# Attention scores of two heads on the two halves of the array's rows, with more buffers for the exponentials, in a fused attention and convolution kernel

## The chip, the cores and the metric

The kernel runs on one core of a Trainium2 chip. The metric is the time of one execution on the device in microseconds, as the median of several executions. Beside the times there is a profile: one execution recorded by the hardware profiler, instruction by instruction, for the engines TensorE (PE; its weight loads are PEld), VectorE (DVE), ScalarE (ACT) and GpSimd (POOL), for the SyncE queue (SP) that issues DMAs, and for the DMA queues.

## The reference

Two layers on an input of 4 images, 128 channels, 64 x 64 pixels, all in float32. The first is self-attention with group normalization, 4 heads of 32 channels, over the 4096 pixels of an image; the second is a residual block of two 3 x 3 convolutions with weights quantized to 3 bits and batch normalization over all images.

```python
# layer 0
x_norm = _group_norm(x, norm_w, norm_b)                   # 8 groups
qkv = einsum('oc,bchw->bohw', qkv_w, x_norm) + qkv_b
q, k, v = split(qkv, 3, axis=1)                           # 4 heads, d = 32
attn = softmax(einsum('bhid,bhjd->bhij', q, k) * d ** -0.5)
out = einsum('bhij,bhjd->bhid', attn, v)
x = x + einsum('oc,bchw->bohw', proj_w, out) + proj_b
# layer 1
out = relu(batchnorm(conv3x3(x, lsq_quantize(w1, alpha1))))
out = batchnorm(conv3x3(out, lsq_quantize(w2, alpha2)))
return relu(out + x)
```

## The kernel before

The attention works on 32 blocks: image b (4 of them) and a chunk of 512 queries qb (8 an image). A block has 32 steps; a step takes 128 keys (kt) and all four heads. For each step TensorE forms the scores s of 128 keys by 512 queries for each head, ScalarE takes their exponential into a tile p of 128 x 2048, TensorE multiplies p with v and accumulates acc over the steps, and p is added up over the steps for the softmax's denominator: most steps by VectorE (r), some by a DMA that accumulates into another tile (rm). The scores are not rounded to the short mantissa of the fast float32 format: q and k are split into a high and a low part, and all four products are summed. Before, the four parts of one head (4 x 32 rows) are stacked on the 128 rows of the array, so one product with K=128 gives one head's scores.

```python
kpool = ctx.enter_context(tc.tile_pool(name="kpool", bufs=NB + 1))        # NB = 8
pss = ctx.enter_context(tc.tile_pool(name="pss", bufs=3, space=PSUM))     # scores, 2 x 512
psa = ctx.enter_context(tc.tile_pool(name="psa", bufs=2, space=PSUM))     # acc, l, po, pk, pq, pv
...
ppool = att.enter_context(tc.tile_pool(name="ppool", bufs=6))
rpool = att.enter_context(tc.tile_pool(name="rpool", bufs=1))

def stack_tile(name):
    return kpool.tile([P, HEADS, FB], F32R, name=name, tag="k")           # 128 x 2048
...
def project_parts(b, j, xin, wide=False):       # q, k, v of one chunk of 512 pixels
    ...
    def parts(what, bias, slot):
        hi = stage.tile([P, FB], F32R, name=f"{what}h{b}_{j}", tag=f"{what}h")
        lo = stage.tile([P, FB], F32R, name=f"{what}l{b}_{j}", tag=f"{what}l")
        nc.scalar.activation(hi, ps[what], AF.Identity, bias=bias)
        nc.vector.scalar_tensor_tensor(lo, ps[what], bias, f32(hi), ALU.add, ALU.subtract)
        nc.sync.dma_start(out=kq[b, j][slot], in_=f32(hi))
        nc.sync.dma_start(out=kq[b, j][slot + 1], in_=f32(lo))
    ...
    return [normalize, lambda: mm("k", P), lambda: parts("k", bk, 0),
            lambda: mm("q", 0), lambda: parts("q", bq, 2), mmv, evac_v]

def load_stack(t, b, j, slots):                 # k: (0, 1, 0, 1), q: (2, 2, 3, 3)
    for s, slot in enumerate(slots):
        nc.sync.dma_start(
            out=f32(t)[s * D : (s + 1) * D, :, :],
            in_=kq[b, j][slot].rearrange("(h d) n -> d h n", d=D))
...
MOVED = range(0, NK - 4, 4)                     # NK = 32

def scores(pair):
    ...
    s = pss.tile([P, 2, FB], F32, name=f"s{n}_{kt}_{half}", tag="s")
    for i in range(2):
        h = 2 * half + i
        nc.tensor.matmul(s[:, i, :], k[:, h, c0 : c0 + P], q[:, h, :], start=True, stop=True)
    nc.scalar.activation(pts[step][:, 2 * half : 2 * half + 2, :], s, AF.Exp, scale=SCALE)

def weights(step):
    ...
    for h in range(HEADS):
        nc.tensor.matmul(acc[n][h * D : (h + 1) * D, :], v[:, kt % KB, h * D : (h + 1) * D],
                         pt[:, h, :], start=(kt == 0), stop=(kt == NK - 1))
    if kt in MOVED:
        if kt == 0:
            msum[n] = rpool.tile([P, HEADS, FB], F32, name=f"rm{n}", tag="rm")
            nc.sync.dma_start(out=msum[n], in_=pt)
        else:
            nc.gpsimd.dma_start(out=msum[n], in_=pt, accum_op=ALU.add)
    elif kt == 2:
        rsum[n] = rpool.tile([P, HEADS, FB], F32, name=f"r{n}", tag="r")
        nc.vector.tensor_tensor(rsum[n], pts[step - 1], pt, ALU.add)
    elif kt > 2:
        nc.vector.tensor_tensor(rsum[n], rsum[n], pt, ALU.add)
```

The end of a block (l: the denominator from r and rm; its reciprocal; po: the output projection) and the projections of the next image's chunks are put between the steps of a block by a list of places; TensorE runs the scores one to two steps ahead of the products with v:

```python
def chunk(b, j, kt, fs, loads):                 # fs: what project_parts returns
    add(kt, "", fs[0])
    add(kt, "q", fs[1])
    add(kt + 1, "", fs[2])
    add(kt + 1, "q", fs[3])
    add(kt + 2, "", fs[4])
    add(kt + 2, "q", fs[5])
    add(kt + 3, "", fs[6])
    ...
# next image's chunks by block: two in blocks 2 and 3, one in 4 to 7
for j, kt in {2: ((0, 13), (1, 22)), 3: ((2, 13), (3, 22)), 4: ((4, 15),), ...
...
run_scores(2)
while at["step"] < steps:
    for s, w in ((3, 1), (3, 2)):
        run_scores(s)
        run_weights(w)
```

The convolutions take bands of 16 rows, two products' groups j of 8 rows each in one PSUM tile of 2 x 512:

```python
for m, (b, g) in enumerate(bandlist):
    ps = done[m] if m < len(done) else conv_tile(i, b, g)
    for j in range(2):
        if m >= len(done):
            conv(ready[i, b, g], ps, j, wq[i])            # 18 products into ps[:, j, :]
        if j == 0:
            prepare(m)
        c = 2 * g + j
        dst = cv[b][:, c * FB : (c + 1) * FB]
        nc.scalar.copy(dst, ps[:, j, :])
        nc.vector.bn_stats(st[:, b * NB + c, :], ps[:, j, :])
```

Of the kernel before, what the change touches and what calls it, by code (L numbers as in the profile page):

```python
# [78 lines left out]
def _fast_body(ctx, tc, x, norm_w, norm_b, qkv_wt, qkv_b, proj_wt, proj_b,  # L79
# [62 lines left out]
    def quant_tasks(pool):  # L142
        tasks = []
        for i, (w, alpha) in enumerate(((w1, alpha1), (w2, alpha2))):
# [19 lines left out]
            for c in range(3):  # L164


                def taps(i=i, c=c, w=w, t=t):
                    wr, q0, qh, ql = (
                        pool.tile([P, FB], F32R, name=f"{n}{i}{c}", tag=tag).bitcast(F32)
                        [:, : 3 * P].rearrange("p (t o) -> p t o", o=P)  # L170
                        for n, tag in (("wr", "kh"), ("q0", "kl"), ("qh", "qh"), ("ql", "ql")))
                    nc.sync.dma_start(out=wr, in_=w[:, 3 * c : 3 * c + 3, :])
                    nc.vector.tensor_scalar(q0, wr, t["inv"], -8.0, ALU.mult, ALU.max)
                    nc.vector.tensor_scalar(q0, q0, 8.0, None, ALU.min)
                    nc.vector.tensor_scalar(qh, q0, SPLIT, None, ALU.add)
                    nc.vector.tensor_scalar(qh, qh, SPLIT, None, ALU.subtract)
                    nc.vector.tensor_tensor(ql, q0, qh, ALU.subtract)
                    nc.vector.scalar_tensor_tensor(wr, qh, t["a_h"], wr, ALU.mult, ALU.subtract)
                    nc.vector.scalar_tensor_tensor(wr, qh, t["a_l"], wr, ALU.mult, ALU.add)
                    nc.vector.scalar_tensor_tensor(wr, ql, t["a_h"], wr, ALU.mult, ALU.add)  # L180
                    nc.vector.scalar_tensor_tensor(wr, ql, t["a_l"], wr, ALU.mult, ALU.add)
                    nc.vector.scalar_tensor_tensor(q0, wr, t["ninv"], q0, ALU.mult, ALU.add)
                    nc.vector.tensor_scalar(q0, q0, QN, QP, ALU.max, ALU.min)
                    nc.vector.tensor_scalar(q0, q0, ROUND, None, ALU.add)
                    nc.vector.tensor_scalar(wq[i][:, 3 * c : 3 * c + 3, :], q0, ROUND, None,
                                            ALU.subtract)

                tasks.append(taps)
# [11 lines left out]
    y0 = [dram.tile([P, N], F32, name=f"y0_{b}") for b in range(B)]  # L200
    att = ExitStack()
# [4 lines left out]
    ppool = att.enter_context(tc.tile_pool(name="ppool", bufs=6))  # L206
    rpool = att.enter_context(tc.tile_pool(name="rpool", bufs=1))

    def stack_tile(name):
        return kpool.tile([P, HEADS, FB], F32R, name=name, tag="k")  # L210
# [50 lines left out]
    kq = {}  # L261
    qs, ks, vs = {}, {}, {}

    def project_parts(b, j, xin, wide=False):
        xn = xpool.tile([P, FB], F32, name=f"xn{b}_{j}", tag="x")
        kq[b, j] = dram.tile([5, P, FB], F32, name=f"kq{b}_{j}")
        ps = {}

        def bank(what):
            if wide:  # L270
                t = pss.tile([P, 2, FB], F32, name=f"p{what}{b}_{j}", tag="s")
                return t[:, 0, :]
            return psa.tile([P, FB], F32, name=f"p{what}{b}_{j}", tag="a")

# [8 lines left out]
        def parts(what, bias, slot):  # L283
            hi = stage.tile([P, FB], F32R, name=f"{what}h{b}_{j}", tag=f"{what}h")
            lo = stage.tile([P, FB], F32R, name=f"{what}l{b}_{j}", tag=f"{what}l")
            nc.scalar.activation(hi, ps[what], AF.Identity, bias=bias)  # L286
            nc.vector.scalar_tensor_tensor(lo, ps[what], bias, f32(hi), ALU.add, ALU.subtract)  # L287
            nc.sync.dma_start(out=kq[b, j][slot], in_=f32(hi))
            nc.sync.dma_start(out=kq[b, j][slot + 1], in_=f32(lo))
# [7 lines left out]
        def evac_v():  # L297
            v = stage.tile([P, FB], F32, name=f"vst{b}_{j}", tag="v")
# [3 lines left out]
            nc.sync.dma_start(out=kq[b, j][4], in_=v)  # L302

        return [normalize, lambda: mm("k", P), lambda: parts("k", bk, 0),
                lambda: mm("q", 0), lambda: parts("q", bq, 2), mmv, evac_v]

    def load_stack(t, b, j, slots):
        for s, slot in enumerate(slots):
            nc.sync.dma_start(
                out=f32(t)[s * D : (s + 1) * D, :, :],  # L310
                in_=kq[b, j][slot].rearrange("(h d) n -> d h n", d=D))

    def load_kv(b, j):
        ks[b, j] = stack_tile(f"k{b}_{j}")
        load_stack(ks[b, j], b, j, (0, 1, 0, 1))
        v = vs[b, j] = vpool.tile([P, KB, P], F32, name=f"v{b}_{j}", tag="v")
        nc.sync.dma_start(out=v.rearrange("p i f -> p (i f)"), in_=kq[b, j][4])

    def load_q(b, j):
        qs[b, j] = qpool.tile([P, HEADS, FB], F32R, name=f"q{b}_{j}", tag="q")  # L320
        load_stack(qs[b, j], b, j, (2, 2, 3, 3))
# [4 lines left out]
    MOVED = range(0, NK - 4, 4)  # L326


    def scores(pair):
# [8 lines left out]
        for i in range(2):  # L338
            h = 2 * half + i
            nc.tensor.matmul(s[:, i, :], k[:, h, c0 : c0 + P], q[:, h, :], start=True, stop=True)  # L340
# [25 lines left out]
    def finish_parts(n):  # L366
# [10 lines left out]
        def total():  # L377
# [5 lines left out]
            t["ls"] = stage.tile([P, FB], F32, name=f"ls{n}", tag="v")  # L383
# [26 lines left out]
    BR = 2 * RB  # L410

    def band_tile(name):
        return (stack_tile(name).rearrange("p h n -> p (h n)")[:, : (BR + 2) * PW]
                .rearrange("p (r w) -> p r w", w=PW))
# [31 lines left out]
    PRE = 3  # L446
    halves = [stack_tile(f"xh{i}") for i in range(2)]
    for j in range(NB):
        eng = (nc.sync, nc.scalar)[j % 2]
        eng.dma_start(out=f32(halves[j // 4])[:, j % 4, :], in_=x_chunk(0, j))  # L450
    st = small.tile([P, NB, 6], F32, name="st0", tag="st")
    for j in range(NB):
        nc.vector.bn_stats(st[:, j, :], f32(halves[j // 4])[:, j % 4, :])
# [3 lines left out]
    def first_chunk(j, wide):  # L457
        return project_parts(0, j, lambda: f32(halves[j // 4])[:, j % 4, :], wide)

    for j in range(PRE):  # L460
        for f in first_chunk(j, True):
            f()
        load_kv(0, j)
        if j == 0:
            load_q(0, 0)

    def schedule(n, before):
# [6 lines left out]
        if before:  # L476
# [5 lines left out]
            add(11, "", before["store"])  # L482
# [5 lines left out]
        def chunk(b, j, kt, fs, loads):  # L488
            add(kt, "", fs[0])
            add(kt, "q", fs[1])  # L490
            add(kt + 1, "", fs[2])
            add(kt + 1, "q", fs[3])
            add(kt + 2, "", fs[4])
            add(kt + 2, "q", fs[5])
            add(kt + 3, "", fs[6])
            if loads:
                add(kt + 3, "", lambda: load_kv(b, j))

        if n == 0:
            for j in range(PRE, NB):  # L500
                chunk(0, j, 4 * (j - PRE), first_chunk(j, False), True)
        if b + 1 < B:
# [12 lines left out]
            for j, kt in {2: ((0, 13), (1, 22)), 3: ((2, 13), (3, 22)), 4: ((4, 15),),  # L515
                          5: ((5, 15),), 6: ((6, 15),), 7: ((7, 15),)}.get(qb, ()):
                xt = {}
                add(kt - 4, "", lambda j=j, xt=xt: xt.update({0: load_x(b + 1, j)}))
                chunk(b + 1, j, kt, project_parts(b + 1, j, lambda xt=xt: xt[0]), False)
# [113 lines left out]
    def layer(i, prepare, done):  # L633

        st = mid.tile([P, B * NB, 6], F32, name=f"st{i}")
        for m, (b, g) in enumerate(bandlist):
            ps = done[m] if m < len(done) else conv_tile(i, b, g)
            for j in range(2):
                if m >= len(done):
                    conv(ready[i, b, g], ps, j, wq[i])  # L640
                if j == 0:
                    prepare(m)
# [3 lines left out]
                nc.vector.bn_stats(st[:, b * NB + c, :], ps[:, j, :])  # L646
# [32 lines left out]
    HN = N // 2  # L679
    res = {}  # L680

    def load_res(b, i):
        if b < B - 1:
            t = mid.tile([P, HN], F32, name=f"res{b}_{i}")
        else:
            t = f32(stack_tile(f"res{b}_{i}")).rearrange("p h n -> p (h n)")
# [3 lines left out]
    def second(m):  # L690
        if m + 2 < len(bandlist):
            relu_band(*bandlist[m + 2])
        if m < 2 * B - 2:
            load_res(m // 2, m % 2)

    a2, c2 = layer(1, second, [])
    for i in range(2):
        load_res(B - 1, i)
    Q = N // 4
    for b in range(B):  # L700
        for j in range(4):
            y = res[b, j // 2][:, (j % 2) * Q : (j % 2 + 1) * Q]
            cs = slice(j * Q, (j + 1) * Q)
# [462 lines left out]
```

## Time and profile before

| | |
|---|---|
| time, median of 3 | 3187.3 us (3182.93 to 3188.45) |
| span of the profiled execution | 3177.3 us, mean granted TensorE clock 0.94 |
| busy: TensorE, VectorE, ScalarE, GpSimd | 2731.6, 2196.2, 2099.9, 184.4 us |
| score products (L340) | 4096, 431 ns each in the mean, 1237.5 us busy |
| products with v (L352) | 8192 records, 1084.7 us busy |
| exponentials (L341) | 2048, 1036 ns each, 1927.5 us busy |
| additions of p by VectorE (L364, L362) | 736 and 32, 2284 and 2292 ns each |
| additions of p by DMA (L359) | 192 of 1024 KB, 7.2 us to landing in the median |
| weight loads of the scores | 4096, 194 ns each |

The busy time of an engine is the union of its instructions. Matmuls are pipelined, so their lengths overlap: what a group of them costs is read from the start of one to the start of the next. In a row of the profile's groups stands the line, the engine, the operation, what it writes and reads, the shape and the count, then the busy time and the mean of one, then the time that the engine stood idle just before and what ended it. The chain is followed back from the last instruction, at each step to what released it. A window's row has the busy time of each engine in one stretch.

### The profile page before, as it was taken

To read this page: it belongs to the slowest core of one execution; us is meant where nothing else is said; L and a number is where in the kernel's file an instruction comes from. 1 tells how busy PE (TensorE), PEld (TensorE's weight loads), DVE (VectorE), ACT (ScalarE), POOL (GpSimd) and SP (SyncE) were. 2 spreads that over 40 slices of the span, in tenths; PEclk is the share of its full clock that TensorE was granted. 3 is DMA by queue.
4 is the path that set the end of the run, shared out by engine and by line. 5 is a ranking of instruction groups with operands and counts; after the bars stand their busy time and mean duration, and the time that the engine had idled before them with its cause. 6 is when DMAs were issued, how large, how long until landed. Compare 5 with 4: busy or idle time off the path is not lost.

```text
span 3177.3 us, 36327 instructions
## 1 busy us (share of the span) xinstructions
PE 2731.6 (86%) x14418; PEld 1226.8 (39%) x14418; DVE 2196.2 (69%) x1445; ACT 2099.9 (66%) x2306; POOL 184.4 (6%) x302
## 2 busy tenths in 40 slices
PE   5898889888998888888898788878978999988785
PEld 2333333333333333333343333333333343356563
DVE  3686767765786677766786676766898888863334
ACT  4586777766876677776786677766867888831223
POOL 1000000000000000000000000000000000000000
PEclk8898999998999999999999899988989999999998
DMA  8766555567665655567565555577545556634003
GB/s 244 174 139 151 121 128 131 123 142 173 142 138 124 148 124 125 127 154 177 130 139 123 126 133 124 128 159 173 129 95 107 127 124 131 133 74 121 10 1 133
DMA packets 155123, 413.70 MB, mean 130 GB/s; under 512 B 49649, under 2 KB 50417, under 8 KB 125249
## 3 DMA queue, kind: packets, MB, share of 16 engines
q0 software_dynamic: 28128, 201.67, 31.4%
q1 hardware_dynamic: 126240, 208.58, 24.1%
q8 instruction: 115, 1.88, 0.2%
q10 hardware_dynamic: 576, 1.05, 0.1%
q14 instruction: 64, 0.52, 0.0%
HBM read 117.64 MB, written 58.72 MB: 56 GB/s over the span
## 4 chain that ended last, share of the span: by engine, by line
PE 53%; DMA 24%; ACT 6%; DVE 6%; issue 5%; ACTq 0%; POOLq 0%; POOL 0%; DVEq 0%; SPq 0%
DMA rm<-p 22%; PE s L340 21%; PE acc L352 20%; PE c L583 8%; ACT p L341 5%; DVE r L364 2%; PE l L381 2%; DMA q<-kq 1%; PE pk L281 1%; PE pv L294 1%; DMA k<-kq 1%; PE pq L281 1%; DVE st L646 1%; DVE res L704 1%; ACT cv L645 1%
## 5 line engine op out<-in xcount | busy, mean ns | idle before, releaser
L341 ACT ACTIVATE p<-s 128x1024 f32<-128x1024 f32 x2048 | 1927.5, 1036 | 668.1 <-PE s L340 405.4
L364 DVE TENSOR_TENSOR r<-r,p 128x2048 f32<-128x2048 f32 x736 | 1680.8, 2284 | 182.6 <-ACT p L341 139.2
L340 PE MATMUL s<-q,k 128*128 128x512 f32 x4096 | 1237.5, 431 | 145.4 <-ACT p L341 121.0
L340 PEld LDWEIGHTS s<-q,k 128*128 128x128 f32 x4096 | 712.8, 194 | 976.9 <-ACT p L341 513.7
L352 PE MATMUL acc<-p,v 128*32 128x512 f32 x8192 | 1084.7, 633 | 0.0
L352 PEld LDWEIGHTS acc<-p,v 128*32 128x32 f32 x8192 | 203.1, 112 | 512.6 <-issue 503.0
L359 POOL DMA_DIRECT2D rm<-p x192 | 164.5, 857 | 2573.3 <-ACT p L341 1493.2
L645 ACT COPY cv<-c 128x512 f32<-128x512 f32 x64 | 37.3, 587 | 275.1 <-PE c L583 257.9
L362 DVE TENSOR_TENSOR r<-p,p 128x2048 f32<-128x2048 f32 x32 | 73.3, 2292 | 187.0 <-PE l L381 187.0
L583 PE MATMUL c<-hi,wq 128*128 128x512 f32 x576 | 155.4, 415 | 52.1 <-DVE st L646 46.1
L646 DVE BATCH_NORM_STATS2 st<-c 128x6 f32<-128x512 f32 x64 | 44.7, 698 | 204.2 <-ACT cv L645 203.8
L287 DVE SCALAR_TENSOR_TENSOR kl<-pk,bk,kh 128x512 fp32r<-128x512 f32 x32 | 24.0, 750 | 190.3 <-ACT kh L286 190.3
L583 PE MATMUL c<-lo,wq 128*128 128x512 f32 x576 | 148.1, 401 | 0.0
L583 PEld LDWEIGHTS c<-hi,wq 128*128 128x128 f32 x576 | 108.2, 193 | 94.5 <-DVE st L646 59.4
L583 PEld LDWEIGHTS c<-lo,wq 128*128 128x128 f32 x576 | 108.7, 189 | 29.4
L281 PE MATMUL pk<-xn,wqkv 128*128 128x512 f32 x64 | 49.3, 862 | 82.0 <-ACT xn L277 82.0
L388 DVE RECIPROCAL rc<-ls 128x128 f32<-128x128 f32 x128 | 114.9, 927 | 2.8 <-ACT ls L384 2.8
L287 DVE SCALAR_TENSOR_TENSOR ql<-pq,bq,qh 128x512 fp32r<-128x512 f32 x32 | 24.0, 749 | 115.3 <-ACT qh L286 115.2
L281 PE MATMUL pq<-xn,wqkv 128*128 128x512 f32 x64 | 42.2, 746 | 58.9 <-DVE kl L287 58.9
L294 PE MATMUL pv<-wqkv,xn 128*128 128x128 f32 x256 | 40.5, 307 | 54.4 <-DVE ql L287 54.4
L294 PEld LDWEIGHTS pv<-wqkv,xn 128*128 128x128 f32 x256 | 36.3, 213 | 69.4 <-DVE ql L287 66.6
L281 PEld LDWEIGHTS pk<-xn,wqkv 128*128 128x128 f32 x64 | 13.1, 242 | 92.8 <-ACT xn L277 92.2
(101 smaller groups left out, 605.8 us busy)
## 6 DMA issues: line engine op xcount, KB each, us to landing
rm<-p POOLq DMA_DIRECT2D x192, 1024.0 KB, 7.4
k<-kq SPq DMA_DIRECT2D x128, 256.0 KB, 7.9
q<-kq SPq DMA_DIRECT2D x128, 256.0 KB, 7.1
rm<-p SPq DMA_DIRECT2D x32, 1024.0 KB, 5.6
x<-in_x_dram SPq DMA_DIRECT2D x80, 256.0 KB, 6.1
kq<-kh SPq DMA_DIRECT2D x32, 256.0 KB, 4.0
kq<-kl SPq DMA_DIRECT2D x32, 256.0 KB, 4.4
kq<-qh SPq DMA_DIRECT2D x32, 256.0 KB, 2.0
```

The lines of the kernel that those rows point to most:

```text
L281: nc.tensor.matmul(ps[what], wqkv[:, o : o + P], xn, start=True, stop=True)
L294: nc.tensor.matmul(ps["v"][:, i * P : (i + 1) * P], xn[:, i * P : (i + 1) * P], wqkv[:, 2 * P : 3 * P], start=True, stop=True)
L340: nc.tensor.matmul(s[:, i, :], k[:, h, c0 : c0 + P], q[:, h, :], start=True, stop=True)
L341: nc.scalar.activation(pts[step][:, 2 * half : 2 * half + 2, :], s, AF.Exp, scale=SCALE)
L352: nc.tensor.matmul(acc[n][h * D : (h + 1) * D, :], v[:, kt % KB, h * D : (h + 1) * D], pt[:, h, :], start=(kt == 0), stop=(kt == NK - 1))
L359: nc.gpsimd.dma_start(out=msum[n], in_=pt, accum_op=ALU.add)
L362: nc.vector.tensor_tensor(rsum[n], pts[step - 1], pt, ALU.add)
L364: nc.vector.tensor_tensor(rsum[n], rsum[n], pt, ALU.add)
L388: nc.vector.reciprocal(rc[:, cs], t["ls"][:, cs])
L583: nc.tensor.matmul(ps[:, j, :].rearrange("p (r w) -> p r w", w=W), w[:, tap, :], part[:, j * RB + kh : j * RB + kh + RB, kw : kw + W], sta ...
L645: nc.scalar.copy(dst, ps[:, j, :])
L646: nc.vector.bn_stats(st[:, b * NB + c, :], ps[:, j, :])
```

## The change

Two heads' scores are formed on the two halves of the array's rows. A k stack now holds, on 64 rows, the high and the low part of one head, and on the other 64 rows those of another; q is given twice, once with its high part on all rows and once with its low part, and the two products are accumulated in PSUM (K=64, four products for a pair of heads where there were two). The k stack is half as wide, and the room goes to p: nine buffers instead of six. Of the 32 steps of a block six instead of seven are added up by DMA. The products of a projection (k, q, v) stand three steps apart and are evacuated two steps later, where they stood one step apart and were evacuated right after. A fourth chunk of the first image is projected before the attention begins, and what is staged there lies in buffers of p. In the convolutions both groups of a band come before their copies, and the statistics are taken from the copy in SBUF instead of from PSUM. The residual is loaded in quarters of an image instead of halves, since the k stacks that serve as its buffers are smaller.

```diff
-    ppool = att.enter_context(tc.tile_pool(name="ppool", bufs=6))
+    ppool = att.enter_context(tc.tile_pool(name="ppool", bufs=9))
 ...
     def stack_tile(name):
-        return kpool.tile([P, HEADS, FB], F32R, name=name, tag="k")
+        return kpool.tile([P, KW], F32R, name=name, tag="k")      # KW = 1188
 ...
-    def load_stack(t, b, j, slots):
-        for s, slot in enumerate(slots):
-            nc.sync.dma_start(
-                out=f32(t)[s * D : (s + 1) * D, :, :],
-                in_=kq[b, j][slot].rearrange("(h d) n -> d h n", d=D))
+    def load_k(b, j):
+        k = ks[b, j] = stack_tile(f"k{b}_{j}")[:, : 2 * FB].rearrange("p (g n) -> p g n", n=FB)
+        for s in range(4):
+            i, part = divmod(s, 2)
+            src = kd[b, j][part].rearrange("(g i d) n -> i d g n", i=2, d=D)
+            nc.sync.dma_start(out=f32(k)[s * D : (s + 1) * D, :, :], in_=src[i])
 ...
     def load_q(b, j):
-        qs[b, j] = qpool.tile([P, HEADS, FB], F32R, name=f"q{b}_{j}", tag="q")
-        load_stack(qs[b, j], b, j, (2, 2, 3, 3))
+        q = qs[b, j] = qpool.tile([P, 2, 2, FB], F32R, name=f"q{b}_{j}", tag="q")
+        src = qd[b, j].rearrange("s (g i d) n -> i g d s n", i=2, d=D)
+        for s in range(4):
+            for g in range(2):
+                nc.sync.dma_start(out=f32(q)[s * D : (s + 1) * D, g, :, :], in_=src[s // 2, g])
 ...
-    MOVED = range(0, NK - 4, 4)
+    MOVED = range(0, NK - 6, 5)
 ...
-        for i in range(2):
-            h = 2 * half + i
-            nc.tensor.matmul(s[:, i, :], k[:, h, c0 : c0 + P], q[:, h, :], start=True, stop=True)
+        for part in range(2):
+            for i in range(2):
+                r = slice(64 * i, 64 * (i + 1))
+                nc.tensor.matmul(s[:, i, :], k[r, half, c0 : c0 + P], q[r, half, part, :],
+                                 start=(part == 0), stop=(part == 1))
 ...
-    PRE = 3
-    halves = [stack_tile(f"xh{i}") for i in range(2)]
+    PRE = 4
+    halves = [ppool.tile([P, HEADS, FB], F32, name=f"xh{i}", tag="p") for i in range(2)]
 ...
-            add(11, "", before["store"])
+            add(12, "", before["store"])
 ...
+        def chunk(kt, fs, gap, wait):
+            add(kt - gap, "", fs[0])
+            for i in range(3):
+                add(kt + gap * i, "q", fs[1 + 2 * i])
+                add(kt + gap * i + wait, "", fs[2 + 2 * i])
 ...
-            for j, kt in {2: ((0, 13), (1, 22)), 3: ((2, 13), (3, 22)), 4: ((4, 15),),
-                          5: ((5, 15),), 6: ((6, 15),), 7: ((7, 15),)}.get(qb, ()):
+            for j, kt in {2: ((0, 13), (1, 22)), 3: ((2, 13), (3, 22)), 4: ((4, 17),),
+                          5: ((5, 17),), 6: ((6, 17),), 7: ((7, 17),)}.get(qb, ()):
 ...
-                chunk(b + 1, j, kt, project_parts(b + 1, j, lambda xt=xt: xt[0]), False)
+                chunk(kt, project_parts(b + 1, j, lambda xt=xt: xt[0]), 3, 2)
 ...
                 if m >= len(done):
                     conv(ready[i, b, g], ps, j, wq[i])
-                if j == 0:
-                    prepare(m)
+            prepare(m)
+            for j in range(2):
                 c = 2 * g + j
                 dst = cv[b][:, c * FB : (c + 1) * FB]
                 nc.scalar.copy(dst, ps[:, j, :])
-                nc.vector.bn_stats(st[:, b * NB + c, :], ps[:, j, :])
+                nc.vector.bn_stats(st[:, b * NB + c, :], dst)
 ...
-    HN = N // 2
+    HN = N // 4
```

## The prediction

> **What bounds the kernel now.** I began with the chain that ended last, on the profile's page, because no engine is full (TensorE 86%, VectorE 69%, ScalarE 66%):
>
> ```profile
> PE 53%; DMA 24%; ACT 6%; DVE 6%; issue 5%; ACTq 0%; POOLq 0%; POOL 0%; DVEq 0%; SPq 0%
> DMA rm<-p 22%; PE s L340 21%; PE acc L352 20%; PE c L583 8%; ACT p L341 5%; DVE r L364 2%; PE l L381 2%; DMA q<-kq 1%; PE pk L281 1%; PE pv L294 1%; DMA k<-kq 1%; PE pq L281 1%; DVE st L646 1%; DVE res L704 1%; ACT cv L645 1%
> ```
>
> Half of the path is TensorE, but the accumulating DMAs (rm<-p) hold 22%. A share is an average, so I cut the attention into its 32 query blocks, at the 32 copies of acc into av (159.1 to 2804.0 us, mean 85.3 us a block), and asked for engine times in single blocks (columns: window, length, busy PE, PEld, DVE, ACT, POOL, clock, DMA share, GB/s):
>
> ```profile
> 234.50:330.40 95.90, 82.00 (x423) 33.51 (x422) 64.40 (x39) 63.98 (x72) 5.18 (x6) 0.91 0.53 127
> 677.40:782.10 104.70, 80.28 (x405) 32.77 (x404) 62.45 (x36) 62.26 (x68) 5.16 (x6) 0.85 0.83 189
> 2591.00:2661.40 70.40, 68.03 (x399) 27.89 (x398) 59.23 (x33) 60.40 (x66) 5.11 (x6) 1.00 0.59 128
> ```
>
> The third is a block of the last image, without projections for a next one: 70.4 us, PE busy nearly throughout, full clock. The first projects two chunks and needs 95.9; the second also loads the next image's k: 104.7. So the floor is TensorE at 70.4, and the rest of the mean (85.3 - 70.4 = 15 us a block) is waiting. The timeline of an undisturbed stretch gives the floor's parts:
>
> ```profile
> 2560.25 1.92 PE L352 MATMUL acc<-p,v 128*32 128x512 f32 x16
> 2562.10 1.66 PE L340 MATMUL s<-q,k 128*128 128x512 f32 x6
> 2562.87 5.60 ACT L341 ACTIVATE p<-s 128x1024 f32<-128x1024 f32 x6 [0.59 <-PE s L340]
> 2563.69 1.06 PE L352 MATMUL acc<-p,v 128*32 128x512 f32 x8
> 2564.69 1.82 PE L340 MATMUL s<-q,k 128*128 128x512 f32 x6
> 2566.44 1.92 PE L352 MATMUL acc<-p,v 128*32 128x512 f32 x16
> ```
>
> From start to start, 16 acc take 1.85, 6 scores 1.59, 8 acc 1.00, 6 scores 1.75: 6.19 us for three steps. ScalarE needs 5.60 and waits 0.59 for PE. 32 steps make 66.0; l and po bring it to 70. The chain inside the 95.9 us block shows the waiting:
>
> ```profile
> 246.56 11.21 DMA rm<-p
> 258.31 7.04 DMA rm<-p
> ...
> 270.84 0.59 ACT kh L286
> 271.45 0.76 DVE kl L287
> 272.26 1.17 PE pq L281 x2
> ...
> 282.82 3.57 PE acc L352 x16
> ```
>
> Two kinds: exponentials' buffers held by accumulating DMAs, and a relay k product, ScalarE, VectorE, q product, during which PE stands. Afterwards the 16 acc took 3.57 instead of 1.85: half clock. In the convolutions the chain repeats:
>
> ```profile
> 2875.86 8.88 PE c L583 x36
> 2884.77 0.59 ACT cv L645
> 2885.39 0.71 DVE st L646
> 2886.14 8.88 PE c L583 x36
> ```
>
> **The Trainium skill.** "TensorEngine Tiling (Array Packing)", Key Properties, says that different tiles load weights and multiply in parallel, and that changing the mode drains the array. The trace agrees for column tiles: the four heads' acc products start some 7 ns apart in single records; no row tile is in it. "TensorE: Matmul & The Clock Gate", Measured speedup vs the span model, has about 4 ns per further tile, and its LDWEIGHTS section says that load time follows columns, not rows; here 128 columns took 194 ns and 32 took 112, so K=64 weights should load no faster. HAM oscillation in that page (idle of some 3 us halves the clock) agrees with the 3.57 above.
>
> **The change part by part.**
> Scores. Per half step, two K=128 products become four of K=64, two per half of the rows. If the halves run together, this is again two rounds of about 0.23 us (single records: 0.228 to 0.236 apart). 32 x 32 x 4 = 4096 rounds; 4 ns for the second tile is +16 us, an estimate from the clock-gate page. Nothing is saved on PE; what is bought is room: k stacks of half the columns pay for three more p buffers, and k loads move half the bytes.
>
> Buffers and DMAs. Six p buffers at about 2.1 us a step cover 12.6 us; an accumulating DMA takes 7.2 us in the median, up to 14.5, after its step and its predecessor. In the 95.9 us block the first one landed at 257.8, 23 us into the block; the exp that reuses its buffer (six steps on, issued about 1.5 steps early) wanted it at 8.5 x 2.1 = 18. With nine buffers and p5 as the first, it is wanted 12.5 steps in, at 70.4/32 = 2.2 a step 27.5 us. Six moved tiles instead of seven come 5 x 2.2 = 11 us apart, above the 7 to 9 us between chained ones in the 70.4 us block. So ScalarE's 220.7 us of waits for rm<-p, and what they drag along, should go. VectorE gets one more add a block: 2.29 x 32 = 73 us, beside PE.
>
> Spaced products. Three steps between k, q and v products with evacuation two steps later: the relay (some 8 us with the halved clock after it) leaves the path, and PE's own part stays: pk 0.86 + pq 0.86 + pv 1.1 + joints 0.4 = 3.2 us a chunk.
>
> Blocks, then: plain 70.3 (the shortest, 2733.7 to 2804.0); with group statistics 71.5, an allowance of 1.2; one chunk 73.5; two chunks 76.7. Images 1 to 3 (less the first block): 2 x 70.3 + 3 x 71.5 + 6 x 76.7 + 12 x 73.5 = 1697. Last image: 70.3 + 5 x 70.3, and two blocks that also quantize weights, whose VectorE was busy 85.2 + 70.5 = 155.6; two adds and some waiting make 165: 587. Together 2284, against 2645 now. Added by choice: 36 for VectorE late with kl and ql (3 us in each two-chunk block, 1.5 in each one-chunk block), 15 for q loads at the three changes of image, 30 (1.3%) for odd waits, 16 for row tiles: 2381.
>
> First block. It ends at 159 now. One chunk more is projected ahead, staged in p buffers (now ScalarE waits 10.9 us for a staging DMA), and four instead of five relays remain inside: 130.
>
> Tail. 3177.3 - 2804.0 = 373. The second convolution of each band now waits for the first one's copy and statistics, since they read the same PSUM tile. With both convolutions first and statistics from SBUF, that goes. A band takes 2886.14 - 2875.86 = 10.28; 36 products at 2.15/9 us (timeline) take 8.6. 30 bands x 1.7 = 50; the last copies come 0.6 later: 324.
>
> Sum: 130 + 2381 + 324 = 2835, and 10 for the median run over the profiled span: **2845 us**.
>
> **Rivals.**
> (1) The row halves take turns. No trace line has row tiles with these operands; for it speaks nothing but that. 4096 rounds x 0.23 = +940: about 3790 us.
> (2) VectorE becomes the bound: 25 adds x 2.36 (three took 7.08) = 59.0, reciprocals 3.7, four small operations 2.9, a chunk 2.2: 68 to 70 a block, plus the wait of the first add for l (187 us over 31 blocks, 6 each): 74 to 76. That is at PE's own 73 to 77, so it would give about 2860, and show as PE waiting for kl and r.
> (3) The DMAs stay the limit, since one accumulate must wait for the last and q loads share the engines (share 0.83 in the 104.7 us block, accumulates 12 to 13 us). If half the waits stay: about 2960.
> (4) Only the buffers help and the relays persist, because VectorE lags: 24 chunks x 5 us, about 2960.
>
> **Range and chances.** 2 and 3 set the upper end, a smaller row-tile toll and none of my added waits the lower: 2765 to 3000 holds 8 in 10. Rival 1 is nearly all of the slow side: faster by over 2% 0.87, within 2% 0.04, slower 0.09.
>
> **What would show it.** Score products with pairs a few ns apart and pairs 0.23 us apart (if 0.23 between all four: rival 1); rm<-p out of the chain; blocks of 70 to 77 us with the clock at 0.98 or more; waits of PE for kl and ql near zero; convolution bands of 8.6 us. I am wrong if blocks stay above 80 with rm<-p or r<-p leading the chain, or if weight loads of K=64 show between rounds.

## The result, and the profile after

The changed kernel takes **2852.9 us** in the median (2852.7 to 2855.2), the kernel before beside it 3187.9: a ratio of 0.895, 95% interval 0.893 to 0.897, or 335 us less. The prediction was 2845, range 2765 to 3000.

The profiled execution spans 2851.1 us, at a mean clock of 0.966 (before 0.94). Its chain that ended last, by engine and by line:

```profile
PE 59%; DVE 25%; issue 7%; DMA 4%; ACT 4%; SPq 1%; POOL 0%; DVEq 0%; POOLq 0%; ACTq 0%
PE s L353 24%; PE acc L366 22%; DVE r L378 18%; PE c L597 8%; ACT p L355 3%; PE l L395 2%; DVE r L376 2%; DMA q<-qd 1%; PE pq L291 1%; DVE rc L402 1%; DMA x<-in_x_dram 1%; PE pv L303 1%; PE po L414 1%; PE pk L291 1%; DMA vd<-vst 1%
```

The accumulating DMAs (rm<-p), 22% before, are gone from it. In their place stands not TensorE alone but VectorE: its additions of p (r L378, L376) hold 20%, where they held 2%. So VectorE may be a new second bound. The share alone doesn't show what that costs: the shortest block below, 66.80 us, has 65% of its own chain in r L378.

The waits of the whole kernel (engine, tile and line, what it waited for: us in total, times, longest) say what is left of those named in the prediction:

```profile
ACT p L355 <- PE s L353: 305.2, 278, 9.4
DVE r L376 <- PE l L395: 161.2, 31, 14.4
PE pq L291 <- DVE kst L297: 31.8, 19, 4.2
PE pv L303 <- DVE qst L297: 21.7, 12, 12.5
```

The exponentials' 220.7 us behind rm<-p have no line any more; what is left is their wait for scores, 305.2 us where it was 405.4. TensorE's waits for the small evacuations were 58.9 and 54.4 and are 31.8 and 21.7: halved, not gone.

Stretches of the span, cut as before at the copies of acc into av (columns as in the prediction): the first block, a block with two chunks, another with two chunks, one with group statistics, one that quantizes weights, the last block, and the tail.

```profile
0.00:151.80 151.80, 108.54 (x642) 49.13 (x644) 80.20 (x66) 81.93 (x94) 14.34 (x30) 0.89 0.65 184
232.10:305.70 73.60, 72.77 (x548) 31.73 (x546) 62.42 (x37) 64.46 (x71) 4.33 (x5) 1.00 0.59 144
305.70:387.20 81.50, 77.88 (x574) 32.66 (x572) 69.71 (x43) 66.55 (x75) 4.30 (x5) 1.00 0.57 141
757.10:840.20 83.10, 73.96 (x554) 30.36 (x552) 70.81 (x52) 62.82 (x68) 4.86 (x6) 0.94 0.52 121
1997.70:2086.80 89.10, 73.07 (x526) 29.68 (x524) 74.53 (x98) 60.63 (x66) 4.25 (x5) 0.91 0.45 100
2460.70:2527.50 66.80, 66.20 (x507) 27.24 (x504) 58.47 (x34) 57.33 (x62) 5.11 (x15) 1.00 0.62 129
2527.50:2851.10 323.60, 280.77 (x1171) 218.03 (x1169) 143.54 (x169) 73.21 (x98) 7.07 (x69) 0.94 0.25 76
```

The second line answers the 95.9 us block of the prediction: the same work, now 73.6, PE busy for 72.8 of it at full clock. The fourth and fifth show where time still goes: PE's work is no larger, but it stands for 9 and 16 us, with VectorE busy for 71 and 75 and the clock at 0.94 and 0.91.

Last, the timeline of an undisturbed stretch, to set beside the six lines in the prediction:

```profile
2302.87 1.92 PE L366 MATMUL acc<-p,v 128*32 128x512 f32 x16
2304.73 1.66 PE L353 MATMUL s<-q,k 64*128 64x512 f32 x12
2305.50 4.69 ACT L355 ACTIVATE p<-s 128x1024 f32<-128x1024 f32 x5 [0.60 <-PE s L353]
2306.32 1.06 PE L366 MATMUL acc<-p,v 128*32 128x512 f32 x8
2307.32 1.82 PE L353 MATMUL s<-q,k 64*128 64x512 f32 x12
2309.07 1.49 PE L366 MATMUL acc<-p,v 128*32 128x512 f32 x12
```

Twelve products with 64 rows take the place of six with 128, from start to start in 1.59 and 1.75 us as before: the cycle is 2309.07 - 2302.87 = 6.20 us, against 6.19. In single records the two products of a pair start 3 to 4 ns apart and pairs 0.23 us apart. The halves run together, and hardly anything is paid for it. Over the whole trace there are 543 groups of six pairs between two stretches of acc, and the shortest tenth of them take 1.589 us or less from start to start; of 557 groups of six products before, 1.583; of 557 in the kernel before with the halves alone (below), 1.582. That is 1 ns a pair at most.

### The profile page after: what moved, and what is told of

Its sections match the earlier page's. It is cut to its first block, busy times and chain, and to the rows that moved or that the text cites. A ratio compares the mean times of both kernels' runs of the same rounds, so it can differ in the third digit from the quotient of the medians.

```text
span 2851.1 us, 44488 instructions
## 1 busy us (share of the span) xinstructions
PE 2637.3 (93%) x18514; PEld 1209.7 (42%) x18514; DVE 2263.6 (79%) x1477; ACT 2093.1 (73%) x2306; POOL 156.6 (5%) x270
## 4 chain that ended last, share of the span: by engine, by line
PE 59%; DVE 25%; issue 7%; DMA 4%; ACT 4%; SPq 1%; POOL 0%; DVEq 0%; POOLq 0%; ACTq 0%
PE s L353 24%; PE acc L366 22%; DVE r L378 18%; PE c L597 8%; ACT p L355 3%; PE l L395 2%; DVE r L376 2%; DMA q<-qd 1%; PE pq L291 1%; DVE rc L402 1%; DMA x<-in_x_dram 1%; PE pv L303 1%; PE po L414 1%; PE pk L291 1%; DMA vd<-vst 1%
## 5 line engine op out<-in xcount | busy, mean ns | idle before, releaser
L355 ACT ACTIVATE p<-s 128x1024 f32<-128x1024 f32 x2048 | 1928.3, 1036 | 416.4 <-PE s L353 305.2
L378 DVE TENSOR_TENSOR r<-r,p 128x2048 f32<-128x2048 f32 x768 | 1754.1, 2284 | 80.1 <-ACT p L355 29.4
L353 PE MATMUL s<-q,k 64*128 64x512 f32 x8192 | 1199.0, 419 | 31.1 <-ACT p L355 17.0
L353 PEld LDWEIGHTS s<-q,k 64*128 64x128 f32 x8192 | 708.8, 187 | 809.4 <-ACT p L355 386.1
L366 PE MATMUL acc<-p,v 128*32 128x512 f32 x8192 | 1044.0, 611 | 0.5 <-DVE vst L308 0.5
L373 POOL DMA_DIRECT2D rm<-p x160 | 136.7, 854 | 2320.6 <-ACT p L355 1533.7
L376 DVE TENSOR_TENSOR r<-p,p 128x2048 f32<-128x2048 f32 x32 | 73.3, 2292 | 161.2 <-PE l L395 161.2
L660 DVE BATCH_NORM_STATS2 st<-cv 128x6 f32<-128x512 f32 x64 | 41.2, 686 | 152.7 <-ACT cv L659 152.7
L291 PE MATMUL pq<-xn,wqkv 128*128 128x512 f32 x64 | 40.9, 725 | 31.8 <-DVE kst L297 31.8
L414 PE MATMUL po<-av,wp 128*128 128x512 f32 x64 | 38.8, 689 | 33.5 <-DVE av L405 33.5
L297 DVE SCALAR_TENSOR_TENSOR kst<-pk,bk,kst 128x512 fp32r<-128x512 f32 x32 | 24.0, 749 | 57.3 <-ACT kst L296 57.0
L297 DVE SCALAR_TENSOR_TENSOR qst<-pq,bq,qst 128x512 fp32r<-128x512 f32 x32 | 24.0, 750 | 56.9 <-ACT qst L296 56.0
L303 PE MATMUL pv<-wqkv,xn 128*128 128x128 f32 x256 | 38.8, 298 | 21.7 <-DVE qst L297 21.7
L395 PE MATMUL l<-r,ones 128*32 128x512 f32 x256 | 36.0, 636 | 23.9 <-DVE r L378 23.9
```

The costliest lines, as they stand in the source:

```text
L291: nc.tensor.matmul(ps[what], wqkv[:, o : o + P], xn, start=True, stop=True)
L303: nc.tensor.matmul(ps["v"][:, i * P : (i + 1) * P], xn[:, i * P : (i + 1) * P], wqkv[:, 2 * P : 3 * P], start=True, stop=True)
L353: nc.tensor.matmul(s[:, i, :], k[r, half, c0 : c0 + P], q[r, half, part, :], start=(part == 0), stop=(part == 1))
L395: nc.tensor.matmul(t["l"][h * D : (h + 1) * D, :], ones, r[:, h, :], start=(r is msum[n]), stop=(r is rsum[n]))
L414: nc.tensor.matmul(t["o"], wp, av, start=True, stop=True)
```

## The experiments

The theory after the result was still that of the prediction: the 335 us are three gains, of the buffers (100 to 200), of spaced products (about 120, by the prediction's 24 x 5) and of the bands (50), while the row halves only make room. The rival: the buffers matter little, and the halved k loads and the spacing did what they seem to do. Four kernels undo one part each.

**Six buffers of exponentials instead of nine.**

```diff
-    ppool = att.enter_context(tc.tile_pool(name="ppool", bufs=9))
+    ppool = att.enter_context(tc.tile_pool(name="ppool", bufs=6))
```

> The changed kernel (2853 us) with six p buffers in place of nine. Theory (the exponentials waited for buffers that an accumulating DMA or a late addition held): the waits come back, though there are only six moved tiles a block; 3 to 6 us a block over 31 blocks and more in the first one, where input and staged tiles share these buffers: 2950 to 3060 us, with ScalarE waiting over 100 us for rm and r. Rival (the gain came from the spaced products and the bands, the buffers are hardly used): under 2890 us.

Measured: 2859.1 us, ratio 0.897 (0.895 to 0.898). That is 6 us more than with nine, little beside the spread of its own runs (2853.8 to 2861.7). The theory fell here. The waits for rm<-p, in the list of waits of the kernel before and then in this kernel's:

```profile
ACT p L341 <- DMA rm<-p: 220.7, 78, 9.7
ACT p L355 <- DMA rm<-p: 47.4, 24, 3.8
```

With as few buffers as the kernel before, 47 us of 220.7 remain, and most of those cost nothing at the end. Something else took most of the waits away.

**Small products close together again**, one step apart and evacuated a step later, with everything else as changed.

```diff
-            add(kt - gap, "", fs[0])
-            for i in range(3):
-                add(kt + gap * i, "q", fs[1 + 2 * i])
-                add(kt + gap * i + wait, "", fs[2 + 2 * i])
+            kt += gap == 3 and kt == 17 and -2
+            add(kt, "", fs[0])
+            add(kt, "q", fs[1])
+            add(kt + 1, "", fs[2])
+            add(kt + 1, "q", fs[3])
+            ...
```

> The changed kernel with the k, q and v products of a projection one step apart and evacuated right after, as before. Theory (the relay k product, ScalarE, VectorE, q product stood on TensorE's path, some 8 us for each of 24 chunks): 3000 to 3060 us, PE waiting for kl and ql over 100 us. Rival (with nine buffers PE has other work queued and the relay is hidden): under 2900 us.

Measured: 3010.4 us, ratio 0.943 (0.941 to 0.946): **157 us more**, the largest part of the change. The block that took 73.6 us takes 95.6, at a clock of 0.89; the window of this kernel, same columns:

```profile
237.00:332.60 95.60, 82.08 (x548) 34.02 (x546) 66.70 (x40) 63.93 (x71) 4.32 (x5) 0.89 0.47 116
```

and its waits for the small evacuations are back at the values of before (the last two lines, from the kernel before):

```profile
ACT p L355 <- PE s L353: 459.5, 303, 9.4
PE pv L303 <- DVE qst L297: 57.4, 18, 8.4
PE pq L291 <- DVE kst L297: 56.2, 19, 4.1
PE pv L294 <- DVE ql L287: 54.4, 19, 3.4
PE pq L281 <- DVE kl L287: 58.9, 19, 5.8
```

TensorE waits 60 us longer for these two evacuations, and is busy 72 us longer for the same products (2709.6 against 2637.3), at a mean clock of 0.943 where it was 0.966. Together that is 132 of the 166 us between the two profiled executions (3016.7 and 2851.1). Blocks of the last image, which project nothing, are unchanged (66.6 to 72.0 us for the last four).

**The old order in the convolutions' bands.**

```diff
-            prepare(m)
-            for j in range(2):
+                if j == 0:
+                    prepare(m)
...
-                nc.vector.bn_stats(st[:, b * NB + c, :], dst)
+                nc.vector.bn_stats(st[:, b * NB + c, :], ps[:, j, :])
```

> The changed kernel with the convolution bands as before: each group's copy and statistics right after its 18 products, statistics from PSUM. Theory (30 bands wait 1.7 us each for the first group's statistics): 2900 us, within 8; the bands 10.3 us again. Rival (the wait is made good later, by the copies at the end of a layer): under 2865 us.

Measured: 2909.9 us, ratio 0.913 (0.911 to 0.915), 57 us more, 2 above the range of the theory. The wait that returns, in its list of waits:

```profile
PE c L597 <- DVE st L660: 46.4, 30, 5.4
```

Thirty waits, one a band, of 1.5 us. In the changed kernel this wait is not there, and its chain through the convolutions has no break for 169 products:

```profile
2589.87 40.34 PE c L597 x169
```

**Seven moved tiles instead of six**, with the nine buffers kept.

```diff
-    MOVED = range(0, NK - 6, 5)
+    MOVED = range(0, NK - 4, 4)
```

> The changed kernel with seven moved tiles a block again (every fourth step). It gives 32 additions of 2.29 us, 73 us in all, back from VectorE to the DMAs. Theory A (VectorE, a quarter of the chain after, is now the bound in the blocks with statistics and two chunks): faster, 2800 to 2840 us. Theory B (TensorE is the bound nearly everywhere, VectorE only late at some places): 2835 to 2865 us. Theory C (the DMAs would be the bound again at four steps, 8.8 us, for 7.6 us each): over 2880 us, with ScalarE waiting for rm.

Measured: 2813.0 us, ratio 0.883 (0.881 to 0.884): **40 us less than the change itself**. The part "fewer accumulating DMAs" is a loss. Its chain by line:

```profile
PE s L353 28%; PE acc L366 25%; DVE r L378 13%; PE c L597 8%; PE l L395 2%; ACT p L355 2%; DMA q<-qd 1%; DVE r L376 1%; PE pq L291 1%; PE pk L291 1%; DVE rc L402 1%; PE pv L303 1%; PE po L414 1%; DMA x<-in_x_dram 1%; DMA tk<-in_L_conv_w_dram 1%
```

VectorE's additions fall from 18% to 13% of the path, and no rm<-p comes into it. One addition a block less on VectorE is 32 x 2.284 = 73 us of its time; the kernel gets 40 of them back. ScalarE's waits for rm<-p stay at 0.5 us in all.

The other two corners of this square tell what the buffers are for. **Six buffers and seven moved tiles**, as the kernel before had them (both edits above):

> The changed kernel with six p buffers and seven moved tiles, both as before. Alone, six buffers gave 2859 us and seven moved tiles 2813 us against 2853. Theory (an accumulating DMA every four steps outlasts six buffers; either more buffers or a wider spacing is enough, so neither shows when undone alone): the waits of ScalarE for rm come back, over 120 us, and the time is 2890 to 2980 us. Rival (the buffers never mattered once the products are spaced): 2810 to 2830 us.

Measured: 2850.0 us, ratio 0.893 (0.889 to 0.898), between the ranges of the theory and of the rival. Against the seven moved with nine buffers it is 37 us slower, and the wait shows why:

```profile
ACT p L355 <- DMA rm<-p: 103.9, 61, 4.7
```

with rm<-p at 17% of its chain. So nine buffers are worth 37 us with seven moved tiles and 6 with six; and the two parts together, as the change has them, give nothing: 2850 without both, 2853 with both. All four kernels of the square have the row halves, the smaller k loads and the spacing; what nine buffers would give without these, no run shows.

If neither the buffers nor the fewer DMAs, what took 117 of the 220.7 us of waits away even here? **The row halves alone**, put into the kernel before (six buffers, seven moved, close products, old bands; the k tiles keep their size and are half used, so that no memory is gained):

```diff
-        for i in range(2):
-            h = 2 * half + i
-            nc.tensor.matmul(s[:, i, :], k[:, h, c0 : c0 + P], q[:, h, :], start=True, stop=True)
+        for part in range(2):
+            for i in range(2):
+                r = slice(64 * i, 64 * (i + 1))
+                nc.tensor.matmul(s[:, i, :], k[r, half, c0 : c0 + P], q[r, half, part, :],
+                                 start=(part == 0), stop=(part == 1))
```

> The kernel before (3188 us) with nothing but the scores on the two halves of the rows: k and q in the new arrangement (k tiles keep their old size, half of it unused, so six buffers), everything else as before. Theory (the halves run together, two rounds as before, and only k's loads are halved): 3150 to 3195 us. Rival 1 (the row form itself saves or costs TensorE time): more than 45 us away from 3188.

Measured: 3090.7 us, ratio 0.970 (0.966 to 0.975): 97 us less (94 against the kernel before beside it, 3184.9). That is outside the range of the theory, and by its number in that of the rival, that the row form itself saves TensorE time. **The same with the k loads as large as before**: each k tile again gets all four heads on all its 128 rows, and the products read half of it.

```diff
-            i, part = divmod(s, 2)
-            src = kq[b, j][part].rearrange("(g i d) n -> i d g n", i=2, d=D)
-            nc.sync.dma_start(out=k[s * D : (s + 1) * D, 0:2, :], in_=src[i])
+            src = kq[b, j][s % 2].rearrange("(h d) n -> d h n", d=D)
+            nc.sync.dma_start(out=k[s * D : (s + 1) * D, :, :], in_=src)
...
-                nc.tensor.matmul(s[:, i, :], k[r, half, c0 : c0 + P], q[r, half, part, :],
+                nc.tensor.matmul(s[:, i, :], k[r, 2 * half + i, c0 : c0 + P], q[r, half, part, :],
```

> The kernel before with the scores on the halves of the rows, as in the run with the halves alone (3091 us), but with k loaded in as many bytes as before: all four heads' columns into every 32 rows, of which each half of the array reads those of its own heads. Theory (the halves gained 97 us through k's loads, half the bytes of which shorten the accumulating DMAs beside them, mostly in the last block of an image): 3150 to 3190 us, those blocks 100 us or more again. Rival (the products on the halves themselves, or q's loads in eight pieces, bring the gain): 3080 to 3110 us.

Measured: 3155.6 us, ratio 0.988 (0.986 to 0.991): 33 us less than before. So 65 of the 97 are the bytes of k. TensorE is busy for 2756.8 us here, against 2731.6 in the kernel before, so the row form itself saves it no busy time. The k tiles are loaded while the last block of an image runs; the DMA issues in the first of these blocks (KB each, median us from issue to landing), with the halves alone and then with k in full:

```profile
rm<-p POOLq DMA_DIRECT2D x6, 1024.0 KB, 8.8
k<-kq SPq DMA_DIRECT2D x28, 128.0 KB, 5.2
```

```profile
k<-kq SPq DMA_DIRECT2D x28, 256.0 KB, 9.9
rm<-p POOLq DMA_DIRECT2D x6, 1024.0 KB, 12.8
```

The accumulates, of the same size in both, land after 8.8 us beside small k loads and after 12.8 beside large ones (12.4 in the kernel before). The three such blocks take 88.6, 88.5 and 84.0 us against 108.0, 106.1 and 99.8: 53 of the 73 us between the two profiled executions (3084.3 and 3156.9). The exponentials' waits for rm<-p, again with the halves alone and then with k in full:

```profile
ACT p L344 <- DMA rm<-p: 88.6, 49, 4.3
ACT p L343 <- DMA rm<-p: 147.8, 62, 7.8
```

Before they were 220.7 us. The other 33 us stay open: with k in full the waits are already 73 us shorter than before, and what does that, the q loads in eight pieces or the products on halves, was not parted.

**Are the halves really taken together?** The change issues the two heads in turn, part by part. This kernel issues both parts of one head, and then both of the other:

```diff
-        for part in range(2):
-            for i in range(2):
+        for i in range(2):
+            for part in range(2):
```

> The changed kernel with the four products of a pair of heads issued head by head (both parts on the lower half of the rows, then both on the upper), instead of alternating. Theory (products start in order, each half takes one at a time, and neighbours in order overlap when they are on different halves): the second and third overlap, and so do the fourth and the next pair's first if nothing waits between them; about one more round of 0.23 us in each group of three pairs, 683 groups: 2960 to 3100 us. If nothing overlaps across pairs, three rounds for two, 2048 more rounds: about 3320. If the order does not matter: 2853.

Measured: 2855.4 us, ratio 0.895 (0.891 to 0.899), as with the turns. The theory that the halves overlap only when neighbours in the queue are on different rows expected more, and missed. Single records still come in pairs, 7 to 16 ns apart in one group (the first at 2302.276 and 2302.283 us), with some 0.22 us from pair to pair. A record doesn't name its rows, so how the pairs form in this order isn't shown.

**Later group statistics.** The chain inside the 83.1 us block (start, length, what) shows what holds those blocks up:

```profile
764.12 6.21 DMA x<-in_x_dram
...
771.45 9.67 DMA x<-in_x_dram
...
781.76 2.27 DVE r L378
...
790.09 2.07 PE po L414 x2
792.16 3.27 PE acc L366 x16
```

The statistics stand among VectorE's additions in the first third of the block. Twice VectorE is idle until an x load lands (3.58 and 3.23 us), and the additions and av that follow the statistics start only after that; po comes late; PE stands, and the 16 acc after it take 3.27 us instead of 1.85. Moved nine steps later at the first of the eight loads and two at the last:

```diff
-                    add(3 * j, "", lambda j=j: xs.update({j: load_x(b + 1, j)}))
-                    add(3 * j + 3, "",
+                    add(2 * j + 9, "", lambda j=j: xs.update({j: load_x(b + 1, j)}))
+                    add(2 * j + 12, "",
```

> The changed kernel with the loads and the group statistics of the next image moved from steps 0 to 24 of the second block of an image to steps 9 to 26. Theory (VectorE waits for input loads that stand behind the rm and q DMAs in the SyncE queue, falls behind, and TensorE then waits for it at po; 82 us instead of the 71 to 74 that TensorE needs, in three blocks): those blocks 74 to 77 us, 2825 to 2840 us in all. Rival (VectorE's 68 to 71 us of work in these blocks are the bound wherever they stand): no change within 6 us.

Measured: 2840.4 us, ratio 0.891 (0.887 to 0.895), 12.6 us less; the three blocks (80.3, 83.1, 81.9) take 78.7, 77.8 and 76.3, which is the 12.5.

**Mends together.** Late statistics, seven moved tiles, the quantization of the weights spread over seven blocks instead of two, and the first four chunks' loads issued a chunk later, so that they don't stand in front of the stores:

```diff
-        if b == B - 1 and qb in (1, 2):
-            for i, f in enumerate(qtasks[:7] if qb == 1 else qtasks[7:]):
-                add(12 + 2 * i, "", f)
+        if b == B - 1 and qb < NB - 1:
+            for i, f in enumerate(qtasks[:2] if qb == 0 else qtasks[qb + 1 : qb + 2]):
+                add(18 + 6 * i, "", f)
```

> A version meant to beat both: the changed kernel with seven moved tiles (2813 us alone), the late statistics (2840 alone, 13 less), the weights' quantization spread over seven blocks of the last image instead of two, and the loads of the first four chunks issued one chunk late, so that they do not hold the next chunk's stores behind them in the SyncE queue. Theory (VectorE's lateness and the queue are what is left above TensorE's own 67 to 74 us): blocks 25 to 27 fall from 253 to about 220 us together, the first block ends at 140 to 147 instead of 152, the rest adds up: 2750 to 2780 us. Rival (DMAs at four steps become the limit in the lighter blocks): 2790 us or more.

Measured: 2758.4 us, ratio 0.864 (0.862 to 0.866), 94 us less than the change. The three blocks that the expectation calls 25 to 27 (254.9 us in the change, 252.8 with seven moved tiles alone) take 211.3: 41.5 us for the spreading. With 40 and 12.6 from the runs above that is 94, the whole. VectorE has 26% of this kernel's chain, where it had 25% in the change: once more its share doesn't follow what it costs. The late loads gave nothing: the first block ends at 151.0 instead of 151.8, not at 140 to 147.

**An eighth moved tile** on top (`MOVED = range(0, NK - 3, 4)`):

> The same with eight moved tiles (steps 0, 4 to 28): another 32 additions, 73 us of VectorE, given to the DMAs. Theory A (VectorE is still late in places): 5 to 25 us less than with seven. Theory B (the last accumulate, issued at step 28, lands after the next block's l wants it at step 2, and the chain of accumulates is full): 5 to 60 us more.

Measured: 2750.5 us, ratio 0.862 (0.860 to 0.864), another 8 less; VectorE falls from 26% to 18% of the chain.

**Two queues and an earlier q.** Instead of later, the first four chunks' loads are issued on GpSimd's queue, while the stores stay on SyncE's; and the next image's first q is loaded at step 12, before most of its k, not at 26.

```diff
-        load_k(0, j)
+        load_k(0, j, nc.gpsimd)
...
-            add(26, "", lambda: load_q(b + 1, 0))
+            add(12, "", lambda: load_q(b + 1, 0))
```

> The last version (eight moved tiles, late statistics, spread quantization; 2751 us), with the loads of the first four chunks issued from GpSimd's queue instead of one chunk late from SyncE's, and the first q of the next image loaded at step 12 of an image's last block instead of step 26. Theory (the first block's chain is stores and loads of different chunks behind one another in one in-order queue; and at the end of an image TensorE waits for q issued behind k loads): first block ends at 135 to 146 us instead of 151, the three last blocks of an image 74 to 78 us instead of 79 to 84: 2715 to 2740 us. Rival for the first block (it is the relays of the chunks inside it, one step apart, and the DMAs' own latency): it ends at 148 to 152, and the time is 2733 to 2745 us.

Measured: **2736.2 us**, ratio 0.858 (0.855 to 0.861), the best of all; it computes everything that the reference does. The last blocks of images 1 to 3 take 75.8, 78.7 and 71.8 us (79.4, 83.6 and 80.3 with the late q). The first block ends at 148.7: the second queue is worth 2 us there, where the theory asked for some 5 to 16 and the rival for next to nothing (148 to 152). These four blocks gain 19 us, of which other blocks give 9 back (2742.6 and 2732.4 us in the profiled executions). Its chain:

```profile
PE 71%; DVE 15%; issue 5%; DMA 5%; ACT 2%; SPq 0%; POOL 0%; DVEq 0%; POOLq 0%; ACTq 0%
PE s L353 30%; PE acc L366 27%; DVE r L378 10%; PE c L597 9%; DMA rm<-p 3%; PE l L395 2%; ACT p L355 2%; DVE r L376 1%; DVE rc L402 1%; PE pv L303 1%; PE po L414 1%; PE pq L291 1%; PE pk L291 1%; DMA q<-qd 1%; DVE kst L297 1%
```

TensorE is busy for 2600.2 of 2732.4 us (95%), at a clock of 0.986. With eight tiles the accumulates are just back on the path (3%).

## Why the prediction was right, and where it was not

The number, 2845 for 2852.9, is good to 0.3%, and that is luck: its parts are off by up to 46 us and cancel. Its sum of three, measured: first block 151.8 (predicted 130), blocks 2375.7 (2381), tail 323.6 (324), and the offset to the median is 2, not 10. The blocks by kind, with the allowances put where the prediction meant them:

| blocks | predicted | measured |
|---|---|---|
| 2 plain ones, the first of the second and third image | 140.6 | 138.2 |
| 3 with group statistics | 214.5 | 245.3 |
| 6 with two chunks, 76.7 + 3 | 478.2 | 473.0 |
| 12 with one chunk, 73.5 + 1.5, and 15 for q | 915.0 | 917.4 |
| 8 of the last image | 586.8 | 601.8 |
| odd waits 30, row tiles 16 | 46.0 | - |

- **Scores: right.** Pairs 3 to 4 ns apart, 0.23 us between pairs; rival 1 is out. The toll of 16 us was too much: the cycle has 6.20 us for 6.19. The Trainium skill, "TensorE: Matmul & The Clock Gate", Measured speedup vs the span model, puts some 4 ns on each further tile of one pack, and the offset inside a pair agrees; but over pairs that follow each other 1 ns of it at most shows here, so multiplying it by 4096 rounds was the error. Weight loads take 187 ns with 64 rows (194 with 128), as the prediction had it.
- **Buffers and DMAs: the waits went as predicted, but not for the reason given.** This is the step that failed. It credited nine buffers and six moved tiles with the end of ScalarE's 220.7 us and of what they drag along; undone together in the changed kernel, these two are worth 3 us, of the wrong sign. The row halves alone take 132 of the 220.7 away (59 of them by k's bytes). The 103.9 that are left with six buffers and seven tiles do go with the buffers alone (0.5 with nine), which gives 37 us, but VectorE's addition takes 40 back. "k loads move half the bytes" stands in the step on scores, without a value; it was worth 65 us. And the added additions of VectorE, "73 us, beside PE", were not beside it: 40 came onto the path.
- **Spaced products: right, and undersized.** Rival 4 valued the relays at 24 x 5 = 120 us; undoing the spacing costs 157, nearly half of it as longer busy time at a lower clock. But "near zero" for the waits was wrong: 53.5 us of 113.3 are left.
- **Blocks: the sum right by cancellation.** An allowance of 1.2 us for group statistics should have been 11.5 (245.3 / 3 - 70.3): x loads and VectorE's order were left out. The quantizing blocks took 174.5 for 165, and left work to the next, 80.4 for 70.3. The 46 us of allowances paid for these. Twelve of the 31 blocks after the first take over 80 us, and in five of them (80.3, 81.2, 81.8, 89.1 and 85.4) r L378 has the largest share of the chain, 31 to 67%: one of the signs that the prediction had named for being wrong.
- **First block: wrong by 22 us.** The step counted relays on PE ("four instead of five") and took the stores and loads of the first chunks for hidden. The chain inside the block says otherwise:

```profile
30.10 5.66 DMA vd<-vst
37.16 6.74 DMA vd<-vst
45.30 4.86 DMA vd<-vst
51.20 6.76 DMA kd<-kst
...
61.02 6.94 DMA q<-qd
68.04 5.25 DMA qd<-qst
74.91 2.08 PE pv L303 x8
```

From 30 to 75 us the path is one transfer after another. Staging in p buffers was to end ScalarE's wait of 10.9 us for a staging DMA; it still waits 10.1 us, for qd<-qst. Two orders of the loads changed it by 0.8 and 3.1 us, so the order is not the main cause; whether fewer bytes or another way of staging would, wasn't tried.
- **Tail: right**, 323.6 for 324; undoing it gives 57 for the 50 of the sum. The 169 products above without a break make 8.6 us for a band of 36, as predicted.
- **Rival 2 came true in part**, and its 2860 is as near to the result as 2845. The total can't tell them apart; the runs can: one addition a block moved back to the DMAs gives 40 us, though VectorE's share of the chain alone would not show it. It showed only in part where rival 2 looked for it, at TensorE waiting for the low parts of k and q and for r (53.5 and 23.9 us); the rest stands in stretches of additions in the chain, behind which av and po come late (TensorE's wait for av before po is 33.5 us, 6.5 before). Rival 3 is out for the change as it is (no rm<-p in the chain), and comes back with six buffers and seven tiles (17%).

The parts by single runs: spacing 157, row halves 97 (of which k's bytes 65), bands 57, buffers with fewer moved tiles -3: 308 of 335. They were measured on different kernels and need not add up; the first block's 7 and the parts' help to each other are in the remaining 27. Not undone alone were, among smaller things, the fourth chunk ahead of the attention, the staging in buffers of p, the residual in quarters, and the stores, which now write the high and the low part of k (and of q) with one DMA of 512 KB instead of two of 256.

## What to carry to other kernels

When a wait for DMAs is to go, first ask which other transfers run beside them: halving the k loads shortened the accumulates from 12.8 to 8.8 us and did more than three further buffers, which gave 6 us with six moved tiles and 37 only where more DMAs were to be kept in flight. A producer and a consumer on an engine that must run without gaps belong several steps apart, as the gap is paid twice, in the wait and in the clock after it. And work taken off a DMA onto an engine at 70% is not free: look at what stands behind it in that engine's order (here av and the statistics), not at the engine's share.

## What the runs showed of the hardware

- Two row halves of K=64 carry two products in the time of one (0.23 us a pair of 512 columns), with a toll of 1 ns a pair at most, and whichever of the two orders they are issued in (2853 and 2855 us).
- The first pair of a group of scores after acc stands 0.33 us before the next pair, not 0.23 (2304.729, 2305.065, 2305.294; 0.337 us in the median of 543 groups). The same 0.33 follows the change from the 32-column products to full-array scores in the kernel before (2562.104, 2562.439, 2562.670; again 0.337 in the median of 557), so going over to row halves costs no more than going over to the whole array.
- An accumulating DMA of 1 MB lands after 8.8 us, in the median of six, beside 28 loads of 128 KB, and after 12.8 beside 28 of 256 KB; over the whole kernel before, the 192 of them take 7.4 us (7.2 is the median with the 32 plain copies that start rm).
